# A four-layer graph network on one core: the softmax sums of the attention layers by transposing records, and a bias moved into a norm's offset

## The chip, the core and the metric

The kernel runs on one core of one Trainium2 chip. The metric is device time in microseconds (us) of one execution; the smaller the better. Times before and after are medians of repeated runs. The profile is one further execution, recorded by the hardware profiler, and its own time stands beside those of the runs.

## The reference

Eight samples of 2048 nodes with 128 features go through four layers: two of masked multi-head attention with a feed-forward part (layers 0 and 1), and two graph attention layers (2 and 3). The mask is one 2048 x 2048 adjacency matrix with about 16 neighbours a node. The change touches layers 0 and 1 alone:

```python
Q = (h @ Wq).reshape(B, N, NUM_HEADS, HEAD_DIM)      # 8 heads of 16
K = (h @ Wk).reshape(B, N, NUM_HEADS, HEAD_DIM)
V = (h @ Wv).reshape(B, N, NUM_HEADS, HEAD_DIM)
scores = jnp.einsum('bnhd,bmhd->bhnm', Q, K) / jnp.sqrt(jnp.asarray(HEAD_DIM, jnp.float32))
scores = jnp.where(mask, -jnp.inf, scores)
attn = jax.nn.softmax(scores, axis=-1)
attn_out = jnp.einsum('bhnm,bmhd->bnhd', attn, V).reshape(B, N, OUT_DIM)
x = h + (attn_out @ Wo + bo)
x = _layer_norm(x, ln1_g, ln1_b)
y = jax.nn.relu(x @ W1 + b1) @ W2 + b2
x = _layer_norm(x + y, ln2_g, ln2_b)
```

Two facts of this formula are used by the change. The softmax needs, for each node, sample and head, the sum of the exponentials over the node's neighbours. And the second bias b2 is added to `x + relu(x @ W1 + b1) @ W2`: if b2 is added to x itself, through the offset of the first norm, then the same b2 enters `x @ W1` too, and b1 has to be made smaller by `W1.T @ b2`.

## The kernel before

**Preparation.** In the opening (`start`), VectorE sweeps the adjacency matrix in 16 blocks of 128 rows and finds each node's neighbours; nodes are then sorted by their number of neighbours. In the same sweep a generator `prepare` makes the weights ready, one step of it in some rounds of the sweep. For layers 0 and 1 it centres the output weights and the two biases (`centered`, L246 to L248) and splits each bias into three bf16 rows (`parts`, L233 to L239), so that one bf16 product with a matrix of ones (`ones_bf`) can add the bias to a whole bank of PSUM.

**Blocks and chunks.** After the sort, a block is 128 nodes with lists of nearly the same length. Block 0 has the longest lists, block 15 the shortest (`CAPS`: 29, 23, 21, ... 12, 10 slots). In layers 0 and 1 a chunk is two slots of a block: two gathers by the GpSimd queue (L294) fetch, for each of the 128 nodes, the rows of two neighbours with keys and values of all eight samples. There are 282 chunks in the two layers, two of them "folded" (the few longest lists of block 0, spread over all partitions). A chunk goes through these steps, each of them a step of the generator `attention_chunk`:

1. VectorE multiplies keys by the query (L627).
2. VectorE adds halves of the products (L633); TensorE turns and adds them into the tile `pair` (L308, eight records); ScalarE takes the exponential (L649) into one slot of a ring of `RING` = 8 tiles, `ring`. It lies there with the weights' (slot, sample, head) index on the partitions and the nodes along the row.
3. TensorE turns the weights back (`back`, L653), ScalarE copies them (L657). At the last chunk of a block, or when six chunks have gathered, `block_sums` runs.
4. VectorE multiplies values by the weights (L665).
5. and 6. TensorE adds the turned values of the two slots into the accumulator `acc` (L308, eight records each).

**The sums of weights, before.** `block_sums` takes the exponentials of the chunks that have gathered and multiplies each by `fold_slots`, a matrix that is two unit matrices of 64 on top of each other. This turns a chunk's weights and adds its two slots in one fp32 product with 64 columns of output (L605). If the block has had sums before, they lie in `partial` and are added by a product with the unit matrix. At the block's last chunk ScalarE copies the sums to `block_sum` (L609), takes their logarithm (L616), and starts the generator `scales`: an exponential of the negative logarithm, spread over the 16 features of a head (L695), eight transposes by TensorE and two copies by ScalarE (L706). `scale` is then one over the sum, in the layout of the accumulator.

**The order of the work.** Nothing is scheduled by a planner: the program writes the order of all engines by hand. The loop in `layers` goes over all chunks. In the round of chunk i it issues, in this order: step 3 of chunk i-1; step 6 of the chunk weighed in the round before; then step 1 of chunk i, a slot, step 2 of chunk i, a slot; then `weigh` with steps 4 and 5 of chunk i-2 (and before them `sums`, if that was the last chunk of its block); then one more slot. A slot advances every waiting generator by one step: the scales, the tails of blocks that are done, the loading of lists, and the fetching of gathers. Four slots after the last chunk of a block was weighed, `outputs` multiplies the accumulator by `scale` on VectorE (L688), and two halves of a tail (`attention_tail`) follow as generators among the next chunks.

**The tail.** For four samples at a time: the product with the output weights, the first bias and the residual (L719, L724, L728), a norm on ScalarE, four transposes, the norm's gain and offset by ScalarE (`affine`, with two columns of `col`), the first feed-forward product (L741), its bias and ReLU on ScalarE (columns 4 and 5 of `col`), then into one bank `y`: the second bias by a bf16 product of 512 columns (L752), the centred residual (L757) and the second product (L762), which all accumulate; a second norm follows, transposes, and the projection of the next layer's rows (L511), which the GpSimd queue writes to the next layer's table.

Of the kernel before, what the change touches and what calls it, by code (L numbers as in the profile page):

```python
# [9 lines left out]
F32 = mybir.dt.float32  # L10
# [8 lines left out]
P = 128  # L19
B, N, D = 8, 2048, 128  # L20
NT = N // P
NH = 8
# [7 lines left out]
NB = 8  # L30
# [3 lines left out]
RING = 8  # L34
# [55 lines left out]
def sparse_path(ctx: ExitStack, tc: tile.TileContext, ins: dict, out: bass.AP, flag: bass.AP):  # L90
# [47 lines left out]
    fold_slots = const.tile([P, NB * NH], F32, name="fold_slots")  # L138
    nc.vector.tensor_add(fold_slots, ident[:, : NB * NH], ident[:, NB * NH :])
# [44 lines left out]
    def load(name, shape, src=None):  # L184
        t = const.tile(shape, F32, name=f"w_{name}")
        nc.scalar.dma_start(t, ins[name] if src is None else src)
        return t
# [17 lines left out]
    for l in (0, 1):  # L205
        W[l] = {
            "qkv": load(f"L{l}_qkv", [P, 384]),
            "o": load(f"L{l}_o", [P, D]),
            "1": load(f"L{l}_gnn_W1", [P, FF]),
            "2": load(f"L{l}_w2", [P, 2, D]),  # L210
            "col": load(f"L{l}_col", [P, 6]),
            "row": row(f"L{l}_row", 4 * D).rearrange("p (a b) -> p a b", b=D),
        }
# [36 lines left out]
    def prepare():  # L250

        for l in (0, 1):
            w = W[l]
            nc.vector.tensor_scalar_mul(w["qkv"][:, :D], w["qkv"][:, :D], 0.25)
            centered(w["o"])
            row_z, row_y = w["row"][:, 0, :], w["row"][:, 1, :]
            centered(row_z)
            w["row_z"] = parts(row_z, f"z{l}")
            yield
            for f in range(2):  # L260
                centered(w["2"][:, f, :])
            centered(row_y)
            w["row_y"] = parts(row_y, f"y{l}")
            yield
        for l in (2, 3):
            w = W[l]
            pa = pair
            nc.tensor.matmul(pa[:, :2], w["T"], w["col"][:, 2:4], start=True, stop=True)
            yield
            nc.vector.tensor_copy(w["h"][:, D : D + 2], pa[:, :2])  # L270
            centered(w["h"][:, :D])
# [323 lines left out]
    def block_sums(l, t, box, last):  # L595

        assert written[0] - box["exps"][0][2] < RING
        terms = [(e, fold_slots[: e.shape[0], :]) for e, folded, _ in box["exps"] if not folded]
# [4 lines left out]
        ps = misc()[:, : NB * NH]  # L603
        for i, (a, b) in enumerate(terms):
            nc.tensor.matmul(  # L605
                ps, a, b, start=i == 0, stop=i + 1 == len(terms), skip_group_check=True
            )
        if last:
            nc.scalar.copy(block_sum[:, t, :], ps)  # L609
        else:  # L610
            box["partial"] = small.tile([P, NB * NH], F32, tag="partial", name="partial")
            nc.scalar.copy(box["partial"], ps)
        box["exps"].clear()
        if last:
            box["r"] = small.tile([P, NB * NH], F32, tag="logs", name="logs", bufs=1)
            nc.scalar.activation(box["r"], ps, AF.Ln)  # L616
            threads.append(scales(l, box))

    def attention_chunk(l, c):
# [41 lines left out]
        if c["last"] or len(box["exps"]) == RING - 2:  # L661
            block_sums(l, t, box, c["last"])
# [12 lines left out]
    def sums(l, t, box):  # L675
        if l < 2:
            if t == NT - 1:
# [35 lines left out]
    def attention_tail(l, t, box, i):  # L713
# [25 lines left out]
        for f in range(2):  # L739
# [12 lines left out]
        nc.tensor.matmul(  # L752
            y, ones_bf, wt["row_y"][:, None, :].to_broadcast([P, 4, D]),
            start=True, stop=False, skip_group_check=True,
        )
        for j in range(4):
            nc.tensor.matmul(  # L757
                y[:, j, :], n1T[:, j, :], center, start=False, stop=False,
# [348 lines left out]
    for l in range(4):  # L1107
        per = 2 if l < 2 else 4
        for t, k, ns, folded in pieces(l, per):
# [3 lines left out]
            every.append(c)  # L1113
    now = [0, 0]
# [630 lines left out]
def layouts(inputs):  # L1745
# [5 lines left out]
    for l in (0, 1):  # L1751
        w = {k: a[f"L{l}_gnn_{k}"] for k in _ATTN}

        def heads_last(m):
# [6 lines left out]
            [w["ln1_g"], w["ln1_b"], w["ln2_g"], w["ln2_b"], w["b1"][:P], w["b1"][P:]], axis=1  # L1761
# [34 lines left out]
```

## Time and profile before

| what | us |
|---|---|
| median of 3 runs | 2945.51 (2943.55 to 2946.8) |
| the profiled execution | 2833.26 |
| its span, first to last instruction | 2831.5 |
| opening: sweep, sort, first rows | 0 to about 165 |
| layers 0 and 1 | about 165 to 1918 |
| layers 2 and 3 | about 1918 to 2831 |

The profiled execution is the one in which all durations of this text were recorded; sums of such durations are set against its time, not against the median. In the lists of the profile, a line has the source line, the engine (PE is TensorE's products, PEld its loading of weights, DVE is VectorE, ACT is ScalarE, POOL is GpSimd), the operation, what it writes and reads, and how often; then the busy time, the mean duration of one in ns, and the idle time of the engine just before, with what ended it. In the timeline a line begins with the start and the duration in us. TensorE's durations overlap, since its records are pipelined: what one record costs is the distance from its start to the next one's.

### The profile page before, as it was taken

The page shows a single profiled execution, that of the slowest core. Times are in us where ns is not written, and L with a number is a line of the kernel's source. Part 1 is how long each engine was busy: PE and PEld are TensorE (multiplying, and loading weights), DVE is VectorE, ACT ScalarE, POOL GpSimd, SP SyncE. Part 2 cuts the span into 40 slices and gives each one's busy share as a digit, 9 for nine tenths or more (in the row PEclk, how much of TensorE's full clock was granted, in tenths as well). Part 3 has the DMA queues.
Part 4 walks back from the last instruction along what each step waited for, and adds up shares of the span by engine and source line. Part 5 has one row for each costly group of instructions (what it writes and reads, how often), then busy time and mean ns, then how long its engine had stood idle before and what let it go on. Part 6 is the DMA issues. An engine that isn't in the chain of part 4 may idle for free.

```text
span 2831.5 us, 49678 instructions
## 1 busy us (share of the span) xinstructions
PE 2394.6 (85%) x18176; PEld 2181.0 (77%) x18176; DVE 2520.7 (89%) x2496; ACT 1376.6 (49%) x5021; POOL 1749.0 (62%) x1276
## 2 busy tenths in 40 slices
PE   5867899898899998799989999998567787888885
PEld 4656888787888887688878888887567786787785
DVE  8888999998899896999999899986889997799995
ACT  3511444454455655154445555556346566354554
POOL 1267688678755554646565565563777775677772
PEclk9988999999999999999999999999789888999998
DMA  9698899999989888789999899985999999999994
GB/s 359 249 376 334 353 333 343 379 336 343 382 328 353 322 313 301 312 317 356 347 380 370 342 366 366 349 298 199 356 411 399 400 409 338 343 411 413 405 413 170
DMA packets 197765, 982.13 MB, mean 347 GB/s; under 512 B 30284, under 2 KB 32076, under 8 KB 125520
## 3 DMA queue, kind: packets, MB, share of 16 engines
q0 software_dynamic: 172112, 885.12, 81.2%
q1 hardware_dynamic: 20502, 75.52, 6.9%
q10 hardware_dynamic: 4900, 18.24, 1.7%
q8 instruction: 146, 2.39, 0.3%
q14 instruction: 105, 0.86, 0.1%
HBM read 921.35 MB, written 91.55 MB: 358 GB/s over the span
## 4 chain that ended last, share of the span: by engine, by line
PE 43%; DVE 22%; DMA 14%; issue 7%; ACT 7%; POOL 1%; POOLq 0%; DVEq 0%; ACTq 0%
PE acc L308 14%; DMA kv<-table,lists 11%; DVE kv L627 7%; DVE kv L665 7%; PE pair L308 4%; PE m L762 4%; PE m L741 4%; PE m L315 3%; PE m L511 3%; DVE kv L633 2%; PE m L757 2%; PE m L605 2%; PE m L564 2%; DVE kv L807 2%; PE m L724 2%
## 5 line engine op out<-in xcount | busy, mean ns | idle before, releaser
L294 POOL DMA_INDIRECT kv<-table,lists x938 | 1282.6, 1367 | 681.4 <-PE acc L308 343.4
L308 PE MATMUL acc<-ident,kv 128*128 128x128 f32 x8048 | 1057.5, 285 | 166.9 <-DVE kv L665 90.1
L308 PEld LDWEIGHTS acc<-ident,kv 128*128 128x128 f32 x8048 | 962.4, 149 | 233.9 <-DVE kv L665 114.2
L665 DVE TENSOR_TENSOR kv<-kv,weights 128x2048 f32<-128x2048 f32 (+1 forms) x282 | 626.5, 2222 | 73.0 <-ACT weights L657 72.9
L627 DVE TENSOR_TENSOR kv<-kv,q 128x2048 f32<-128x2048 f32 (+1 forms) x280 | 618.2, 2208 | 48.1 <-DMA kv<-table,lists 31.4
L807 DVE TENSOR_TENSOR kv<-kv,pair 128x3584 f32<-128x3584 f32 (+1 forms) x150 | 530.7, 3538 | 1.0
L308 PE MATMUL pair<-ident,kv 128*128 128x128 f32 (+1 forms) x2256 | 303.7, 279 | 76.4 <-issue 53.0
L633 DVE TENSOR_TENSOR kv<-kv 128x1024 f32<-128x1024 f32 (+1 forms) x282 | 334.8, 1187 | 9.1
L308 PEld LDWEIGHTS pair<-ident,kv 128*128 128x128 f32 (+1 forms) x2256 | 259.5, 142 | 96.1 <-issue 70.4
L294 POOL DMA_INDIRECT kv<-table,sorted_lists x150 | 191.6, 1277 | 147.4 <-PE acc L308 48.3
L657 ACT COPY weights<-pair 128x128 f32<-128x128 f32 (+1 forms) x282 | 73.3, 260 | 394.7 <-PE pair L653 389.5
L474 ACT ACTIVATE n<-m,eps 128x128 f32<-128x128 f32 x512 | 181.1, 370 | 146.3 <-PE m L762 142.0
L812 ACT ACTIVATE kv<-kv,ws 128x128 f32<-128x128 f32 x544 | 174.6, 397 | 155.6 <-DVE ws L801 145.9
L649 ACT ACTIVATE ring<-pair 128x128 f32<-128x128 f32 (+1 forms) x282 | 77.7, 276 | 316.1 <-PE pair L308 253.8
L849 ACT ACTIVATE n<-m,eps 128x128 f32<-128x128 f32 x256 | 90.6, 373 | 178.5 <-PE m L841 176.6
L762 PE MATMUL m<-w_L_w,hT 128*128 128x128 f32 x1024 | 156.3, 275 | 0.0
L481 ACT ACTIVATE n<-m,rs 128x128 f32<-128x128 f32 x512 | 145.9, 374 | 0.3
L741 PE MATMUL m<-n1T,w_L_gnn_W 128*128 128x512 f32 x256 | 133.7, 606 | 7.9 <-ACT hT L746 5.0
L498 POOL DMA_INDIRECT table<-rows,perm x57 | 94.8, 1663 | 68.7 <-ACT own L534 17.3
L762 PEld LDWEIGHTS m<-w_L_w,hT 128*128 128x128 f32 x1024 | 135.0, 192 | 0.0
L315 PE MATMUL m<-ident,n 128*128 128x128 f32 x640 | 114.2, 291 | 13.7 <-ACT n L481 7.4
L511 PE MATMUL m<-w_L_h,xT 128*128 128x130 f32 x512 | 84.8, 298 | 42.7 <-ACT xT L485 27.3
(220 smaller groups left out, 3702.4 us busy)
## 6 DMA issues: line engine op xcount, KB each, us to landing
kept<-xT SPq DMA_DIRECT2D x48, 512.0 KB, 7.2
xT<-kept SPq DMA_DIRECT2D x48, 512.0 KB, 7.1
kv<-in_adj_dram SPq DMA_DIRECT2D x16, 1024.0 KB, 8.8
table<-kv ACTq DMA_DIRECT2D x16, 1024.0 KB, 8.0
kv<-table,lists POOLq DMA_INDIRECT x938, 8.9
kv<-in_x_nodes_dram SPq DMA_DIRECT2D x16, 512.0 KB, 12.6
kv<-table,sorted_lists POOLq DMA_INDIRECT x150, 7.0
found<-cand POOLq DMA_DIRECT2D x16, 64.0 KB, 5.8
```

Source lines behind the costliest of these rows:

```text
L294: this = nc.gpsimd.indirect_dma_start(out=dst, out_offset=None, in_=tables[l][:, :] if need == NT else views[l][0], in_offset=bass.Indirec ...
L308: nc.tensor.matmul(dst, src, ident, start=start, stop=True, is_transpose=True, skip_group_check=True)
L315: nc.tensor.transpose(pt[:, j * P : (j + 1) * P], src[:, j, :], ident)
L474: nc.scalar.activation(dst[:, i, :], z[:, i, :], AF.Square, bias=eps, scale=D**-0.5, accum_out=ss[:, i : i + 1],)
L511: nc.tensor.matmul(pp[:, j, :], xT[:, h + j, :], w["qkv"][:, D:] if l < 2 else w["h"], start=j == 0, stop=True, skip_group_check=True,)
L627: nc.vector.tensor_mul(kk, kk, q[:, None].to_broadcast([P, ns, NB, D]))
L633: nc.vector.tensor_add(hk.rearrange("p j (c h) -> p c j h", h=NH), kj[:, :, :NH, :], kj[:, :, NH:, :])
L665: nc.vector.tensor_mul(vv, vv, w.rearrange("p (s b h) -> p (s b) h", b=NB, h=NH)[:, :, None, :] .to_broadcast([P, ns * NB, HD, NH]),)
L741: nc.tensor.matmul(ph, wt["1"][:, f * P : (f + 1) * P], n1T.rearrange("p b c -> p (b c)"), start=True, stop=True,)
L762: nc.tensor.matmul(y[:, j, :], hT[:, f, j, :], wt["2"][:, f, :], start=False, stop=f == 1, skip_group_check=True,)
L807: nc.vector.tensor_mul(hv[:, :, :nv, :], hv[:, :, :nv, :], wc[:, :, :nv, None].to_broadcast([P, ns, nv, D]))
L812: nc.scalar.mul(hv[:, i, b, :], hv[:, i, b, :], ws[:, i, b - nv : b - nv + 1])
```

## The change

The sums: `fold_slots` goes. `block_sums` now turns each chunk's weights by one transposing record with the unit matrix, into 128 columns, so that the two slots stay side by side; they accumulate in PSUM. It always ends in a copy to `partial`, now 128 columns wide. The halves of `partial` are added by VectorE in `sums`, which runs where the block's last chunk is weighed; the logarithm and the start of `scales` move there from `block_sums`. The ring has nine tiles in place of eight, so `block_sums` runs at seven chunks in place of six; it also runs whenever the next chunk belongs to another block (`leave`).

The bias: `prepare` no longer centres and splits the second bias. It takes b2 as a seventh column of `col`, computes `W1.T @ b2` by two small products into `pair`, subtracts it from the columns of b1 and adds b2 to the offset of the first norm. The bf16 product at the head of `y` goes.

```diff
-RING = 8
+RING = 9
...
-    fold_slots = const.tile([P, NB * NH], F32, name="fold_slots")
-    nc.vector.tensor_add(fold_slots, ident[:, : NB * NH], ident[:, NB * NH :])
...
-            row_z, row_y = w["row"][:, 0, :], w["row"][:, 1, :]
+            row_z = w["row"][:, 0, :]
             centered(row_z)
             w["row_z"] = parts(row_z, f"z{l}")
-            yield
+            pb = pair
+            for f in range(2):
+                nc.tensor.matmul(
+                    pb[:, f : f + 1], w["1"][:, f * P : (f + 1) * P], w["col"][:, 6:7],
+                    start=f == 0, stop=f == 1, skip_group_check=True,
+                )
+            yield
+            nc.vector.tensor_sub(w["col"][:, 4:6], w["col"][:, 4:6], pb[:, :2])
+            nc.vector.tensor_add(w["col"][:, 1:2], w["col"][:, 1:2], w["col"][:, 6:7])
             for f in range(2):
                 centered(w["2"][:, f, :])
-            centered(row_y)
-            w["row_y"] = parts(row_y, f"y{l}")
             yield
...
-    def block_sums(l, t, box, last):
+    def block_sums(t, box, last):
...
-        terms = [(e, fold_slots[: e.shape[0], :]) for e, folded, _ in box["exps"] if not folded]
+        plain = [e for e, folded, _ in box["exps"] if not folded]
+        terms = []
         if "partial" in box:
             terms.append((ident, box["partial"]))
         if last and t == 0:
             terms += [(merge, box["wf"][:, i, :]) for i in range(FOLD)]
-        ps = misc()[:, : NB * NH]
+        ps = misc()[:, :P]
+        for i, e in enumerate(plain):
+            m = e.shape[0]
+            nc.tensor.matmul(
+                ps[:, :m], e, ident[:m, :m], start=i == 0, stop=not terms and i + 1 == len(plain),
+                is_transpose=True, skip_group_check=True,
+            )
         for i, (a, b) in enumerate(terms):
             nc.tensor.matmul(
-                ps, a, b, start=i == 0, stop=i + 1 == len(terms), skip_group_check=True
-            )
-        if last:
-            nc.scalar.copy(block_sum[:, t, :], ps)
-        else:
-            box["partial"] = small.tile([P, NB * NH], F32, tag="partial", name="partial")
-            nc.scalar.copy(box["partial"], ps)
+                ps[:, : b.shape[-1]], a, b, start=False, stop=i + 1 == len(terms),
+                skip_group_check=True,
+            )
+        box["partial"] = small.tile([P, P], F32, tag="partial", name="partial")
+        nc.scalar.copy(box["partial"], ps)
         box["exps"].clear()
-        if last:
-            box["r"] = small.tile([P, NB * NH], F32, tag="logs", name="logs", bufs=1)
-            nc.scalar.activation(box["r"], ps, AF.Ln)
-            threads.append(scales(l, box))
...
-        if c["last"] or len(box["exps"]) == RING - 2:
-            block_sums(l, t, box, c["last"])
+        if c["last"] or c["leave"] or len(box["exps"]) == RING - 2:
+            block_sums(t, box, c["last"])
...
     def sums(l, t, box):
         if l < 2:
+            both = box["partial"]
+            nc.vector.tensor_add(block_sum[:, t, :], both[:, : NB * NH], both[:, NB * NH :])
+            box["r"] = small.tile([P, NB * NH], F32, tag="logs", name="logs", bufs=1)
+            nc.scalar.activation(box["r"], block_sum[:, t, :], AF.Ln)
+            threads.append(scales(l, box))
...
         y = misc().rearrange("p (b c) -> p b c", c=D)
-        nc.tensor.matmul(
-            y, ones_bf, wt["row_y"][:, None, :].to_broadcast([P, 4, D]),
-            start=True, stop=False, skip_group_check=True,
-        )
         for j in range(4):
             nc.tensor.matmul(
-                y[:, j, :], n1T[:, j, :], center, start=False, stop=False,
+                y[:, j, :], n1T[:, j, :], center, start=j == 0, stop=False,
                 skip_group_check=True,
             )
...
+    for c, n in zip(every, every[1:] + [None]):
+        c["leave"] = n is None or n["box"] is not c["box"]
...
-            [w["ln1_g"], w["ln1_b"], w["ln2_g"], w["ln2_b"], w["b1"][:P], w["b1"][P:]], axis=1
+            [w["ln1_g"], w["ln1_b"], w["ln2_g"], w["ln2_b"], w["b1"][:P], w["b1"][P:], w["b2"]],
+            axis=1,
```

More of the change, by code (lines that the diff above doesn't have):

```diff
@@ L210, in sparse_path @@
             "2": load(f"L{l}_w2", [P, 2, D]),
-            "col": load(f"L{l}_col", [P, 6]),
+            "col": load(f"L{l}_col", [P, 7]),
             "row": row(f"L{l}_row", 4 * D).rearrange("p (a b) -> p a b", b=D),
```

## The prediction

> **What bounds the kernel now.** I read the page first, then the table of stretches, then who waits for whom on VectorE (DVE) inside a stretch, then the timeline of one block's end.
>
> ```profile
> span 2831.5 us, 49678 instructions
> ...
> PE 2394.6 (85%) x18176; PEld 2181.0 (77%) x18176; DVE 2520.7 (89%) x2496; ACT 1376.6 (49%) x5021; POOL 1749.0 (62%) x1276
> ```
>
> Over the span DVE leads TensorE (PE) by a little. The change touches only the opening (0 to 165 us) and the two attention layers (165 to 1918 us), so those have to be read alone:
>
> ```profile
> 165.00:600.00 435.00, 365.99 (x2739) 331.63 (x2738) 413.72 (x336) 163.59 (x561) 321.26 (x196) 0.93 0.92 353
> ...
> 800.00:1055.00 255.00, 246.33 (x1915) 221.28 (x1915) 228.66 (x165) 145.82 (x498) 140.49 (x89) 0.99 0.90 340
> ...
> 1600.00:1918.00 318.00, 303.17 (x2470) 275.90 (x2469) 288.14 (x169) 181.91 (x697) 192.37 (x112) 1.00 0.91 345
> ```
>
> Columns: stretch, length, busy PE, PEld, DVE, ACT, POOL, granted clock, DMA share, GB/s. From 165 to 600 us DVE is busy 95% and PE 84%: a chunk costs DVE 2.29 + 1.22 + 2.30 us (L627, L633, L665). In the last blocks of each layer (800 to 1055, 1600 to 1918) PE is busy 97% and 95%, DVE 90%: lists are short there, and the tail, which costs PE the same for every block, weighs more. What DVE waits for in 800 to 1055:
>
> ```profile
> DVE kv L665 <- ACT weights L657: 20.2, 11, 4.1
> ...
> DVE o L688 <- PE acc L308: 1.2, 1, 1.2
> ```
>
> 20.2 us there, and 22.3 us in 1600 to 1918, go to weights that PE turns over late. That is all that a faster PE can win in these two stretches. One end of a block, on DVE:
>
> ```profile
> 934.87 1.23 DVE L665 TENSOR_TENSOR kv<-kv,weights 128x1024 f32<-128x1024 f32 x1 [1.75 <-ACT weights L657]
> 936.01 2.29 DVE L627 TENSOR_TENSOR kv<-kv,q 128x2048 f32<-128x2048 f32 x1
> 938.33 1.22 DVE L633 TENSOR_TENSOR kv<-kv 128x1024 f32<-128x1024 f32 x1
> 943.61 2.29 DVE L665 TENSOR_TENSOR kv<-kv,weights 128x2048 f32<-128x2048 f32 x1 [4.05 <-ACT weights L657]
> ...
> 949.28 1.28 DVE L688 TENSOR_TENSOR o<-acc,scale 128x512 f32<-128x512 f32 x2
> ```
>
> DVE waits 1.75 and 4.05 us for weights, then runs without a gap: PE is the bound up to 943, DVE from there until the next tail.
>
> [...] a product is two records, a transpose one, and records start equally far apart. [...] here 12 sums' records lie 107.5 ns apart and 8 transposes 109 ns:
>
> ```profile
> 1013.26 1.45 PE L605 MATMUL m<-fold_slots,ring 128*128 128x64 f32 x12
> 1014.55 1.04 PE L308 MATMUL acc<-ident,kv 128*128 128x128 f32 x8
> 1015.42 1.03 PE L308 MATMUL pair<-ident,kv 128*128 128x128 f32 x8
> ...
> 1017.06 0.38 PE L752 MATMUL m<-parts_y,ones_bf 128*128 128x512 bf16 x1
> 1017.28 0.39 PE L757 MATMUL m<-center,n1T 128*128 128x128 f32 x2
> ```
>
> [...] The trace has that shape once, at 215 ns:
>
> ```profile
> L139 DVE TENSOR_TENSOR fold_slots<-ident 128x64 f32<-128x64 f32 x1 | 0.2, 215 | 0.0
> ```
>
> **The change, part by part.**
>
> *PE, sums.* 280 chunks (282 less two folded) give 560 records; each becomes one: 560 x 107.5 - 280 x 109 ns = 29.7 us less. Partial sums: 30 products now. With a flush at seven chunks or on leaving a block, counted through the loops, 57 flushes take the place of 62 and 25 carry a partial: 60 x 108 - 50 x 111 ns, 0.9 us less.
>
> *PE, bias.* 64 L752 records go, each 0.22 us of PE (1017.06 to 1017.28): 14.2 us. In all 44.8 us of PE.
>
> *Where that counts.* In the block shown, PE loses 12 + 4 sum records (925.42 to 926.70 and 934.44 to 935.07, 1.91 us) and gains 7 (0.76), and loses two L752 (0.44): 1.6 us before the second wait. The eight transposes of scale (0.88 us), now ahead of it, move behind it. So the weights come 2.5 us earlier. Blocks 9 to 15 of layer 0 and 8 to 15 of layer 1, 15 in all, show such waits: at most 42.5 us, 2.8 a block. Elsewhere PE waits for DVE, L665 above all, and its gain is hidden by DVE's three products per chunk; if DVE were quicker it would count.
>
> *DVE, sums.* 32 adds of 128x64, 0.13 us (start to next start after L139) to 0.215 us each. In the 17 blocks where DVE is the bound they are on the path: 2.2 to 3.7 us, taken 3.5; in the others they lie inside the wait for weights. The add waits for ACT's copy of the partial; behind it in DVE's queue stands L665 of the same chunk, which needs weights copied about 1 us earlier. Where DVE leads, this costs L665 up to 1 us, but PE wants that product only 5 us later (946.58); I take 0, with 0 to 0.3 us a block for the range.
>
> *ACT.* 62 copies of 212 ns become 57 of 264 ns (L657's row, same shape): 1.9 us more on an engine at 49%, taken 0. Ln and the scale's Exp move from the step after the weights to the weighing step, over one chunk later. Ln waits for the DVE add, and ACT's queue behind it holds a tail's row copies; the add has long run, so no new wait there. No DMA moves; SP's and POOL's order is the same.
>
> *The wait that comes.* Scale used to be ready 5.2 us before L688 at 949.28. Now, counting from the turned weights at 942.55: the second row copies end about +3.7, Ln .23 and Exp 1.07 take it to +5; transposes at +5.1 to +5.5; the tail's projection, whose input sits behind Exp on ACT, to +7.3; the chunk's eight transposes .87, scale's second four .44, two ACT copies of .6 with a row copy between: about +10. L688 stood at +6.7, so it comes 3.4 us later from there, against 2.5 us gained: a net +0.9 in such a block. In layer 1, blocks 8 to 10, the weights' waits are 1.5 to 2.3 us and no projection lies in that chunk: scale is ready near +7.5, and about 1.5 us is kept. Between these I take 0.8 us kept a block: 15 x 0.8 = 12 us. Where DVE is the bound, 5.65 us of DVE work lie between L633 and L688 and scale needs 2.6 us: hidden.
>
> *Opening.* Centring and splitting the second bias runs on DVE from 43.53 to 46.21 us and again for layer 1, in a stretch where DVE has no gap: 5.4 us go. A subtraction and an addition of 2 and 1 columns (near L247's 150 ns) add 0.35 us a layer. Net 4.6 us. The subtraction waits for two new products; PE has a whole round of the sweep (6 us) for them: taken 0, up to 2 us a layer.
>
> *Between the layers* (1055 to 1300 us) the wait for weights is 21.1 us in six pieces, and q another 5.2; I take 3 us.
>
> Sum: -4.6 + 3.5 - 12 - 3 = -16 us against the profiled execution's 2833.3 us (span 2831.5): about 2817. The median of the runs, 2945.5, lies 4.0% above that execution; scaled alike, -16.7, about 2929. Why they differ the profile doesn't show: with a slower PE the gain would grow, with slower DMA shrink.
>
> **Rivals.**
>
> *PE's gain is kept whole.* For it: 42.5 us of waits name PE. Against it: scale's later place. 15 x 2.5 = 37 us in place of 12: -41, 2902.
>
> *Hidden.* DVE at 95% and DMA at 0.92 set the pace, scale's lateness eats the gain: -4.6 + 5.5 for all adds, about +1, 2946. For it: DVE runs gapless after 943. Against it: the 97% of PE.
>
> *Slower: scale comes late.* Its place is L688 in the 15 late blocks; it decides once the chain from the turned weights to scale's second copy passes about +9.2 us, where the 2.5 us are used up. At +11 each block loses 1.8 us: 27 us, with the other terms (-4.6 + 3.5 - 3) +23, 2969; at +10, +9, 2955. For it: my own count for the worst blocks is +10. Against it: layer 1's blocks, and transposes of scale that move into chunks where PE has less to do.
>
> *The change does not halve the records*: excluded nearly, since every transpose in the trace is one record.
>
> **How the numbers follow.** Chances: forecast 0.48, kept whole 0.2, hidden 0.16, slower 0.16. The range 2902 to 2952 holds the forecast with its bounds (scale, adds, the subtraction's wait), the whole gain, the hidden case, and part of the slower one. A measurement can tell about 0.2% (5.9 us) from no change: faster 0.69, same 0.15, slower 0.16.
>
> **What would show it.** Right: half as many sum records, no L752; DVE's wait for weights in the late blocks well under 42 us, and a new wait of L688 for scale, 1 to 3 us each in those blocks; the opening some 4 us shorter. Wrong: L688 waits over 4 us a block (slower), or none at all (kept whole); or L627 waiting for gathers instead.

## The result: 1.2% faster, twice the forecast

| | us |
|---|---|
| kernel before, median of 4 runs beside the changed one | 2944.53 (2941.18 to 2946.8) |
| changed kernel, median of 4 runs | 2910.26 (2906.23 to 2913.36) |
| ratio, with its 95% interval | 0.9884 (0.9867 to 0.9901) |
| the changed kernel's profiled execution, and its span | 2913.36, 2911.6 |

The change takes 34.3 us away; the forecast was 16.5, from 2945.5 to 2929. The sign was right and the result lies in the range, but the size was off by a factor of two. The terms for the opening and for the late blocks came out as forecast; one step, on the early blocks, had the mechanism wrong, and it makes up the whole difference.

The two profiled executions can't be set against each other by their spans: 2831.5 us before, 2911.6 after, although the runs say that the changed kernel is the faster one. The first experiment shows why: layers 2 and 3, which the change doesn't touch, took 895 us in the first trace of the kernel before and 1009 in its second. So everything below is read from the opening and the two attention layers, up to the product with `scale` of layer 1's last block (L688 before, L698 after). Its first half begins at 1936.8 us in the first trace of before, at 1935.1 in the second, and at 1901.3 in the trace after. The difference there is 33.8 or 35.5 us, as much as the runs show.

The changed kernel's busy times, then one group of instructions of the kernel before and three of the changed one:

```profile
PE 2406.4 (83%) x17830; PEld 2161.2 (74%) x17830; DVE 2521.9 (87%) x2507; ACT 1378.2 (47%) x5016; POOL 1714.2 (59%) x1276
```

```profile
L665 DVE TENSOR_TENSOR kv<-kv,weights 128x2048 f32<-128x2048 f32 (+1 forms) x282 | 626.5, 2222 | 73.0 <-ACT weights L657 72.9
```

```profile
L670 DVE TENSOR_TENSOR kv<-kv,weights 128x2048 f32<-128x2048 f32 (+1 forms) x282 | 626.1, 2220 | 24.5 <-ACT weights L662 14.4 <-ACT rs L468 9.0 <-ACT rs L469 1.1
L632 DVE TENSOR_TENSOR kv<-kv,q 128x2048 f32<-128x2048 f32 (+1 forms) x280 | 618.1, 2207 | 33.7 <-DMA kv<-table,lists 28.0 <-ACT q L573 5.7
...
L683 DVE TENSOR_TENSOR block_sum<-partial 128x64 f32<-128x64 f32 x32 | 7.6, 239 | 15.9 <-ACT partial L621 6.7 <-ACT weights L662 4.7 <-ACT n L478 2.3
```

TensorE has 346 instructions fewer (18176 before): 280 records of sums, 10 of partial sums and 64 bias products went, 8 records for the product of W1 and b2 came. VectorE has 11 more: 32 new adds, less what the opening lost. The product with the weights, L665 before and L670 now, waits 24.5 us in all, where it waited 73.0; the new add (L683) waits 15.9. The profile puts one product's wait down to now one, now another operation of ScalarE (`weights`, `rs`, `n`), the one that ended last, so waits are compared here by these totals of the waiting operation.

One of the stretches of the prediction (stretch, length, busy PE, PEld, DVE, ACT, POOL, granted clock, DMA share, GB/s):

```profile
800.00:1055.00 255.00, 243.16 (x1874) 214.92 (x1873) 229.76 (x169) 151.74 (x528) 136.98 (x86) 1.00 0.89 339
```

Here, in late blocks, TensorE is busy 95% where it was 97%, VectorE 90% as before. In the first stretch of the prediction, 165 to 600, the trace has the products with the weights of 71 chunks, where it had those of 70, and six of the new adds besides. That is a first hint that time was won where the prediction had none to win.

The end of the block that the prediction showed, on TensorE and then on VectorE (start, duration, and in brackets the idle time before it and what ended that):

```profile
916.88 1.08 PE L611 MATMUL m<-ident,ring 128*128 128x128 f32 x7
917.89 1.09 PE L312 MATMUL acc<-ident,kv 128*128 128x128 f32 x8
```

```profile
918.29 0.23 DVE L683 TENSOR_TENSOR block_sum<-partial 128x64 f32<-128x64 f32 x1 [0.73 <-ACT partial L621]
918.44 1.22 DVE L670 TENSOR_TENSOR kv<-kv,weights 128x1024 f32<-128x1024 f32 x1
...
925.18 2.29 DVE L670 TENSOR_TENSOR kv<-kv,weights 128x2048 f32<-128x2048 f32 x1 [2.06 <-ACT rs L468]
...
932.64 0.69 DVE L698 TENSOR_TENSOR o<-acc,scale 128x512 f32<-128x512 f32 x1 [1.70 <-ACT scale L716]
```

Seven turns take 1.01 us from 916.88 to the next record at 917.89 (the prediction had 0.76), in place of 12 + 4 records before. The two waits for weights of 1.75 and 4.05 us have become a wait of 0.73 for the partial sums and one of 2.06. And the wait that the prediction announced is there: L698 waits 1.70 us for the second half of `scale`.

In the opening, two operations of 0.15 us with no wait ahead of them (L264 and L265, at 43.46 and 43.53 us) stand where centring and splitting the second bias took 2.7 us.

### The profile page after: what moved, and what is told of

Its sections match the earlier page's. It is cut to its first block, busy times and chain, and to the rows that moved or that the text cites. A ratio compares the mean times of both kernels' runs of the same rounds, so it can differ in the third digit from the quotient of the medians.

```text
span 2911.6 us, 48942 instructions
## 1 busy us (share of the span) xinstructions
PE 2406.4 (83%) x17830; PEld 2161.2 (74%) x17830; DVE 2521.9 (87%) x2507; ACT 1378.2 (47%) x5016; POOL 1714.2 (59%) x1276
## 5 line engine op out<-in xcount | busy, mean ns | idle before, releaser
L298 POOL DMA_INDIRECT kv<-table,lists x938 | 1268.0, 1352 | 785.8 <-PE acc L312 343.2
L312 PE MATMUL acc<-ident,kv 128*128 128x128 f32 x8048 | 1097.3, 289 | 210.5 <-issue 93.5
L312 PEld LDWEIGHTS acc<-ident,kv 128*128 128x128 f32 x8048 | 980.1, 150 | 294.0 <-issue 148.7
L670 DVE TENSOR_TENSOR kv<-kv,weights 128x2048 f32<-128x2048 f32 (+1 forms) x282 | 626.1, 2220 | 24.5 <-ACT weights L662 14.4
L632 DVE TENSOR_TENSOR kv<-kv,q 128x2048 f32<-128x2048 f32 (+1 forms) x280 | 618.1, 2207 | 33.7 <-DMA kv<-table,lists 28.0
L824 DVE TENSOR_TENSOR kv<-kv 128x1024 f32<-128x1024 f32 x75 | 91.6, 1222 | 70.9 <-ACT kv L818 56.8
L698 DVE TENSOR_TENSOR o<-acc,scale 128x512 f32<-128x512 f32 x128 | 83.3, 684 | 67.0 <-PE acc L312 29.2
```

The lines of the kernel that those rows point to most:

```text
L298: this = nc.gpsimd.indirect_dma_start(out=dst, out_offset=None, in_=tables[l][:, :] if need == NT else views[l][0], in_offset=bass.Indirec ...
L312: nc.tensor.matmul(dst, src, ident, start=start, stop=True, is_transpose=True, skip_group_check=True)
L632: nc.vector.tensor_mul(kk, kk, q[:, None].to_broadcast([P, ns, NB, D]))
L670: nc.vector.tensor_mul(vv, vv, w.rearrange("p (s b h) -> p (s b) h", b=NB, h=NH)[:, :, None, :] .to_broadcast([P, ns * NB, HD, NH]),)
```

## The experiments

The theory after the result: **TensorE's time counts in every block, not in the late ones alone**, because TensorE makes the query and the weights that VectorE waits for, and perhaps because it frees the buffers that the next gathers need. The rivals: the surplus comes from the sums' new order or from the ring's ninth tile; or from the bias; or it is no gain of the attention layers at all, but of layers 2 and 3. Four sets of kernels were run, each set on one chip with the kernel before beside it. Ratios are to that kernel before, and "the mark" is the start of the last block's L688 or L698 of layer 1 in the trace.

### The kernel before, once more (before_again)

No edit; one run with its profile.

> The kernel before, unchanged, for a second trace of it. The first trace is 4% shorter than the timed runs, and its layers 2 and 3 took 895 us from the last L688 of layer 1 to the end, those of the changed kernel 1010 us. Theory: the difference between the profiled execution and the runs lies in layers 2 and 3 alone, so this trace has its last L688 of layer 1 near 1937 us again and ends near 2942 us. Rival: the two attention layers are slower too in ordinary runs, and that L688 comes near 1970 us or later; then the gain read between the first two traces is not the gain of the runs.

It took 2946.34 us, with a span of 2944.5. The mark lies at 1935.1 us, 1.7 from the first trace's. Layers 2 and 3 in the first trace of before, then in the second:

```profile
1918.00:2831.00 913.00, 701.51 (x5446) 664.29 (x5444) 777.49 (x924) 471.58 (x1855) 601.33 (x565) 0.89 0.92 359
```

```profile
1918.00:2944.00 1026.00, 753.54 (x5440) 691.23 (x5440) 777.38 (x922) 469.23 (x1849) 589.75 (x564) 0.84 0.87 319
```

The same work of VectorE (777 us) takes 113 us longer, with TensorE at a lower granted clock (0.84 against 0.89). So the 4% between the first profile and the median, which the prediction could not explain, lie in layers 2 and 3. Two traces of one kernel differ by up to 2 us at the mark; single stretches between blocks differ by up to 3.5.

### The two halves, each alone (bias_alone, sums_alone)

The first has the bias's part of the change and the old sums. The second has the new sums, with the old ring of eight, and keeps the bias product.

```diff
 bias_alone
-        nc.tensor.matmul(
-            y, ones_bf, wt["row_y"][:, None, :].to_broadcast([P, 4, D]),
...
 sums_alone
-            nc.tensor.matmul(
-                ps, a, b, start=i == 0, stop=i + 1 == len(terms), skip_group_check=True
-            )
+            nc.tensor.matmul(
+                ps[:, :m], e, ident[:m, :m], start=i == 0, stop=not terms and i + 1 == len(plain),
+                is_transpose=True, skip_group_check=True,
+            )
...
```

> Only the second bias is moved; the sums stay as before. Theory (TensorE's time counts in nearly every block, because its backlog also delays the gathers): 14.2 us of PE records and 4.6 us of DVE in the opening go, about 2.6 us of the opening and 9 us of the rest are won: 2933 us (-12). Rival of the prediction (PE's time counts only in the 15 late blocks): -2.6 and 15 x 0.44 = 6.6 us: 2935. Rival that it is the sums which matter alone: -3.

> Only the sums are changed, with a ring of eight tiles (flush at six chunks), and the bias product stays. Theory: 30.6 us of PE go, and about two thirds of it are won, -20 us: 2924. Rival of the prediction (late scales give most of it back, nothing in blocks that DVE bounds): -8 to +4 us: 2937 to 2948.

The bias alone took 2922.15 us beside 2944.11, ratio 0.9935 (0.9915 to 0.9955), the sums alone 2927.96, ratio 0.9938 (0.9914 to 0.9962). At the mark they are 17.0 and 16.3 us ahead of before_again; together 33.3, against 33.8 for the whole change. The halves simply add up.

The opening is worth 4.7 us of it. To the first product with `scale` it is 269.2 us, the mean of the eight traces with the bias's part and the tail in its place (after, bias_alone, ring8, pe_twice, dve_five, pe_early, pe_late and scales_at_once), and 273.9 in the three without (the two of before, and sums_alone). So 12.3 of the bias's 17.0 us were won in the attention layers, where it takes away 64 products of 0.22 us, 14.2 in all. A change that only removes TensorE time there kept most of it, and 34 of the 64 products belong to the 17 blocks where the prediction had put TensorE's gain down as hidden. The gain is not spread evenly: against before_again it is 0.9 us up to block 8 of layer 0, which is within the scatter of single stretches, and 6.2 us up to block 8 of layer 1.

### The ring with eight tiles (ring8)

```diff
-RING = 9
+RING = 8
```

> The changed kernel with eight ring tiles: block_sums runs at six chunks again, 4 or 5 more partial sums of two records each per layer (1.1 us of PE a layer) and an ACT copy of 264 ns each. Both theories: within 0.1% of the changed kernel (2910), at most +3 us. If the burst of seven turns is what helps, it is slower by more than 5 us.

2911.21 us beside 2944.11, ratio 0.9888 (0.9848 to 0.9927), the mark at 1899.3: as the changed kernel. The ninth tile, and with it the number of flushes, brings nothing that can be seen.

### TensorE's gain given back (pe_twice)

Every turn of the sums is issued twice, the second time starting the accumulation anew. This adds 280 records, at 109 ns each 30.5 us.

```diff
-        for i, e in enumerate(plain):
+        for i, e in enumerate(plain + plain):
...
-                ps[:, :m], e, ident[:m, :m], start=i == 0, stop=not terms and i + 1 == len(plain),
+                ps[:, :m], e, ident[:m, :m], start=i % len(plain) == 0,
+                stop=not terms and i + 1 == 2 * len(plain),
```

> The changed kernel with every transposing record of the sums issued twice (the second round overwrites the first, so the result is the same): 280 more records of 109 ns, 30.5 us of PE, with the order and the late scales of the changed kernel. Theory (PE's time counts nearly everywhere, the gathers' buffers included): two thirds of it come back, +20 us: 2930, and L632's wait for gathers and L670's for weights rise to those of before. Rival of the prediction (PE counts only in the 15 late blocks, about 1 us each): +12 to +15 us in the late blocks and nothing before block 8 of layer 0.

2934.89 us beside 2944.38, ratio 0.9968 (0.9951 to 0.9985). The mark comes 25.3 us later than in the changed kernel, for 30.5 us of records at 109 ns, or 34.6 by their busy time in the trace (77.6 us where the changed kernel has 43.0). Of this, 10.0 us lie between block 0 and block 8 of layer 0, where the prediction had TensorE hidden. This kernel also says what the sums' new order costs: its TensorE has the load of bias_alone, and its mark comes 8.5 us after bias_alone's (1926.6 and 1918.1). So of the sums, some 25 us are won by fewer records and some 8.5 are given back by the adds, the later scales and what follows from them, each known to the 2 us by which two traces of one kernel differ.

### Four more adds a block (dve_five)

```diff
+            for _ in range(5):
-            nc.vector.tensor_add(block_sum[:, t, :], both[:, : NB * NH], both[:, NB * NH :])
+                nc.vector.tensor_add(block_sum[:, t, :], both[:, : NB * NH], both[:, NB * NH :])
```

> The changed kernel with the add of the halves issued five times: 128 more adds of 0.13 us (issue distance) to 0.215 us on DVE. If DVE is the bound in 17 of 32 blocks, as the prediction says, half of them are on the path: +9 to +15 us, 2920 to 2925. Theory now (DVE had gaps of 1 to 6 us a block there too, which end with PE or a gather): the first adds vanish in gaps, +4 to +9 us, 2914 to 2919. If DVE is the bound in all blocks: +17 to +27 us.

2932.07 us beside 2944.38, ratio 0.9966 (0.9951 to 0.9981); the mark is 21.3 us later than in the changed kernel. Five adds in succession cost more than the expectation allowed, as the end of one block shows:

```profile
922.86 1.27 DVE L684 TENSOR_TENSOR block_sum<-partial 128x64 f32<-128x64 f32 x5 [0.73 <-ACT partial L621]
924.04 1.22 DVE L670 TENSOR_TENSOR kv<-kv,weights 128x1024 f32<-128x1024 f32 x1
```

From 922.86 to the next product it is 1.18 us, where the single add took 0.15 (918.29 to 918.44): 0.26 us for each added one. Over the trace their starts lie 0.25 to 0.32 us apart, so that the 128 adds are 33.7 us of VectorE, not 17 to 27, and 63% of them arrive at the mark (78% with the opening left out, which in this trace came out 4.3 us shorter). They arrive by stage: 9.0 us up to block 8 of layer 0 and 9.3 up to block 8 of layer 1, for 8.4 us of adds in each; 6.3 us in the late blocks of layer 1 and none in those of layer 0, for 7.4 us in each. So VectorE is on the path in the early blocks, as the prediction said. What it had wrong is that TensorE was not. (The logarithm takes the last add's result, so that scale may come up to 1 us later too, an estimate from four adds of 0.26 us; that part is not told apart.)

### TensorE loaded in the early or in the late blocks (pe_early, pe_late)

This is the test of the step itself. Blocks 0 to 7 of both layers, or blocks 8 to 15, get 336 more records, 36.6 us at 109 ns each.

```diff
+        times = 3 if t < 8 else 1
-        for i, e in enumerate(plain):
+        for i, e in enumerate(plain * times):
```

For pe_late the first line reads `times = 4 if t >= 8 else 1`.

> The changed kernel with the sums' transposing records of blocks 0 to 7 of both layers issued three times: 168 chunks, 336 more records of 109 ns, 36.6 us of TensorE, all in the blocks that the prediction called bound by DVE. If DVE hides TensorE's time there (the prediction): at most 5 us slower than the changed kernel, ratio to before 0.988 to 0.990. If TensorE's time counts there too (what pe_twice suggests): 25 to 37 us slower, ratio 0.997 to 1.001.

> The same amount of TensorE in the other half: records of blocks 8 to 15 of both layers issued four times, 112 chunks, 336 more records, 36.6 us. Both the prediction (a PE-bound stage) and the theory of pe_twice expect most of it on the path: 28 to 37 us slower than the changed kernel, ratio to before 0.998 to 1.001. If the wait for scale is what sets these blocks, more: over 37 us.

By the busy time of these records in the traces the load is more than 36.6 us: 43 in pe_early and 39 in pe_late (82.3 us where the changed kernel has 43.0). The changed kernel, then pe_early:

```profile
L611 PE MATMUL m<-ident,ring 128*128 128x128 f32 (+1 forms) x280 | 43.0, 279 | 0.0
```

```profile
L612 PE MATMUL m<-ident,ring 128*128 128x128 f32 (+1 forms) x616 | 86.1, 280 | 0.0
```

| | us, before 2927.74 | ratio | mark, later than the changed kernel |
|---|---|---|---|
| pe_early | 2917.29 | 0.9959 (0.9937 to 0.9982) | 22.9 of 36.6 to 43 us |
| pe_late | 2931.07 | 1.0008 (0.9991 to 1.0025) | 38.9 of 36.6 to 39 us |

The ratios say the same as the marks: set against 0.9884, they are 22 and 36 us. In the late blocks all of TensorE's time counts; in the early ones 53 to 63% of it, with 12.8 us more up to block 8 of layer 0 and 9.8 up to block 8 of layer 1. Neither "hidden" (5 us or less) nor "the whole" describes the early blocks.

The added records stand directly ahead of VectorE's add, so a rival is that they cost time only through that place, which the kernel before did not have. In pe_early it is not so. Its groups, to be set beside those of the changed kernel above:

```profile
L634 DVE TENSOR_TENSOR kv<-kv,q 128x2048 f32<-128x2048 f32 (+1 forms) x280 | 618.0, 2207 | 48.3 <-DMA kv<-table,lists 25.9 <-ACT q L573 16.5 <-PE pair L660 2.6
L672 DVE TENSOR_TENSOR kv<-kv,weights 128x2048 f32<-128x2048 f32 (+1 forms) x282 | 626.0, 2220 | 32.9 <-ACT weights L664 16.3 <-ACT rs L468 9.4 <-ACT rs L469 6.0
...
L685 DVE TENSOR_TENSOR block_sum<-partial 128x64 f32<-128x64 f32 x32 | 7.4, 233 | 16.5 <-ACT partial L623 14.1 <-ACT rs L468 2.3
```

The add waits 16.5 us in place of 15.9. What grew is the wait of the product with the query (from 33.7 to 48.3 us, though the gathers' share of it fell from 28.0 to 25.9) and of the product with the weights (from 24.5 to 32.9): VectorE waits for things that TensorE now makes later. In pe_late the place does matter; there the add waits 29 us more than in the changed kernel:

```profile
L685 DVE TENSOR_TENSOR block_sum<-partial 128x64 f32<-128x64 f32 x32 | 7.5, 235 | 45.1 <-ACT partial L623 30.7 <-issue 5.1 <-ACT rs L469 4.6
```

### The tail placed a slot later (outputs_later)

```diff
-range(4 if l < 2 else 3 if t > NT - 4 else 5)
+range(5 if l < 2 else 3 if t > NT - 4 else 5)
```

> The changed kernel with one more yield ahead of outputs: L688's successor (L698) then stands behind the next weights' product L670 on DVE, not ahead of it. In the changed trace DVE waits 26.8 us at L698 for scale, 9.9 of it at the change of layers. Theory (the wait is idle time of DVE that PE's late blocks mostly hide): the wait falls under 8 us and the time by 3 to 10 us: 2900 to 2907. Rival (the tail starts one slot later and its burst on PE moves into the next block): no gain or up to +10 us: 2910 to 2920.

If late scales cost much, giving them one slot more should help. 2948.59 us beside 2944.38, ratio 1.0018 (1.0002 to 1.0034), and the mark 37.8 us later than in the changed kernel. VectorE's waits in the two attention layers, the changed kernel first, then this one:

```profile
DVE o L698 <- ACT scale L716: 26.8, 18, 9.9
...
DVE kv L632 <- ACT q L573: 5.7, 6, 1.9
```

```profile
DVE kv L670 <- ACT weights L662: 37.8, 16, 7.0
DVE kv L632 <- ACT q L573: 33.0, 14, 4.5
...
DVE o L698 <- ACT scale L716: 9.6, 9, 1.7
```

The wait for scale fell from 26.8 to 9.6 us, as intended. But the wait for the query grew by 27 us, and that of the product with the weights from 24.5 us to 37.8. That the tail's work now meets the query's and the weights' on TensorE and ScalarE is argued from this, not tested.

### Scale started at once, and the tail sooner (scales_at_once, outputs_sooner, both_sooner, before_sooner)

scales_at_once takes the generator's first step where it is made, so that the exponential stands one slot earlier. outputs_sooner puts the tail one slot earlier; both_sooner does both; before_sooner does it in the kernel before.

```diff
 scales_at_once
-            threads.append(scales(l, box))
+            turning = scales(l, box)
+            next(turning)
+            threads.append(turning)
 outputs_sooner, before_sooner
-range(4 if l < 2 else 3 if t > NT - 4 else 5)
+range(3 if l < 2 else 3 if t > NT - 4 else 5)
```

> The changed kernel with the first step of the scales (ScalarE's Exp) issued in the weighing step itself and not in the slot after it, so that the whole chain to scale comes one slot sooner. In the changed trace DVE waits 26.8 us at L698 for scale. Theory (late scales cost part of the gain): that wait falls below 15 us and the time by 4 to 10 us, 2900 to 2906. Rival (scale's lateness is hidden behind other waits, or its transposes now stand on TensorE ahead of an Exp that is not done): within 3 us of the changed kernel, or up to 10 us slower.

> The changed kernel with one yield less ahead of outputs, so L698 and the tail come one slot sooner. One slot later cost 38 us, mostly as waits of L632 for the next block's query. Theory A (the tail's burst on TensorE must be clear of the query's products): sooner is better, L632's waits for q vanish (5.7 us) and 3 to 10 us are won unless L698 waits for scale. Theory B (scale is ready only just before L698 now): L698's wait rises by about 2 us in each of the 15 late blocks and the kernel is 10 to 30 us slower than the changed one, 2920 to 2940.

> Scales one slot sooner and outputs one slot sooner together. If the lateness of scale (theory B) is all that hurts outputs_sooner, this one is as fast as the changed kernel or up to 10 us faster, 2900 to 2912. If the place of the tail itself hurts, it is slower than the changed kernel like outputs_sooner.

> The kernel before with one yield less ahead of outputs; its scale is ready 5 us ahead of L688, so no wait for scale comes in. It shows what the place of the tail is worth by itself. Theory A: 3 to 10 us faster than before (2934 to 2941). Theory B: L688 waits for the last accumulation instead in the late blocks (it waits 8 us already), 0 to 15 us slower.

| | us, before 2832.05 | ratio |
|---|---|---|
| scales_at_once | 2801.15 | 0.9878 (0.9849 to 0.9908) |
| outputs_sooner | 2879.76 | 1.0162 (1.0139 to 1.0186) |
| both_sooner | 2883.67 | 1.0169 (1.0147 to 1.0192) |
| before_sooner | 2882.47 | 1.0163 (1.0137 to 1.0188) |

On this chip layers 2 and 3 ran as in the first trace, so the times stand some 110 us lower; the ratios are what is compared. scales_at_once is the changed kernel again (its interval holds 0.9884, and its mark is 2.2 us earlier). Its wait for scale, then the totals of the weights' product and of the add:

```profile
DVE o L700 <- ACT scale L718: 25.2, 12, 9.4
```

```profile
L670 DVE TENSOR_TENSOR kv<-kv,weights 128x2048 f32<-128x2048 f32 (+1 forms) x282 | 626.0, 2220 | 25.9 <-ACT weights L662 25.8
...
L683 DVE TENSOR_TENSOR block_sum<-partial 128x64 f32<-128x64 f32 x32 | 7.6, 237 | 17.2 <-ACT partial L621 17.2
```

Scale is waited for 12 times in place of 18, but for nearly as long, 25.2 us after 26.8; the other two totals were 24.5 and 15.9. So moving the exponential alone does not bring scale sooner where it is waited for, and the 8.5 us that the new order costs were not won back. Which part of them is the add's wait and which is scale's stays open.

The other three lose 1.6 to 1.7%, with or without the earlier scale, and in the kernel before as well. There, again the waits of VectorE in the attention layers, before_again first, then before_sooner:

```profile
DVE kv L665 <- ACT weights L657: 47.3, 32, 6.9
DVE kv L665 <- ACT rs L464: 16.8, 6, 4.1
...
DVE kv L627 <- ACT q L569: 12.7, 8, 3.3
```

```profile
DVE kv L665 <- ACT weights L657: 78.9, 34, 4.5
DVE kv L627 <- ACT q L569: 63.1, 19, 5.4
```

The query's wait is five times as long; that of the product with the weights, of which before_again has 6.5 us more under another name, grew from 70.6 to 78.9 us. For the changed kernel four slots is the best of the three places tried: one slot sooner it loses 2.9% (1.0162 over the 0.9878 of scales_at_once), one slot later 1.4% (1.0018 over 0.9884).

## What the prediction had right, and the step that failed

**The working, term by term**, against the trace after (time between the products with `scale`, L688 or L698), from the first trace of before, on which the prediction was built, and from the second:

| term | predicted, us | from the first trace | from before_again |
|---|---|---|---|
| opening | -4.6 | -2.6 (-4.7 over the eleven traces named above) | -0.5 |
| 17 blocks "where DVE is the bound" | +3.5 | -9.9 (layer 0), -6.6 (layer 1) | -13.4, -5.0 |
| 15 late blocks | -12 | -5.6 (layer 0), -6.8 (layer 1) | -4.0, -6.9 |
| between the layers | -3 | -4.0 | -4.0 |
| sum | -16 | -35.5 | -33.8 |

The stretches are not quite the prediction's blocks: block 0 lies in the opening or between the layers, and block 8 of layer 1 among the early ones. With it among the late ones, layer 1 reads -5.9 and -7.6 from the first trace, which changes nothing of what follows.

Apart from the 17 blocks, the terms lie within about 2 us of the forecast. **The failed step** is the sentence "Elsewhere PE waits for DVE, L665 above all, and its gain is hidden by DVE's three products per chunk", and the +3.5 us drawn from it. In place of a loss of 3.5 us these blocks gave 16.5 (18.4 from before_again): the term was 20 us too high, which is the whole surplus. TensorE's time there was not hidden; pe_early puts the part that counts at 53 to 63%. The rival of a gain "kept whole" meant something else, 37 us from the late blocks alone; those gave 12.4, and that the total came near that rival's was luck.

Why the step failed is to be read in the same profile. The prediction read 95% busy as "the bound" and listed VectorE's waits in the late blocks only. Up to block 8 of layer 1, before and after, they are these:

```profile
DVE kv L665 <- ACT weights L657: 15.8, 9, 5.0
DVE kv L627 <- ACT q L569: 8.0, 6, 1.9
```

```profile
DVE kv L632 <- ACT q L573: 5.4, 5, 1.9
DVE kv L670 <- ACT weights L662: 3.9, 3, 2.3
DVE o L698 <- ACT scale L716: 2.9, 1, 2.9
DVE block_sum L683 <- ACT rs L468: 2.2, 1, 2.2
```

23.8 us of waiting for things that TensorE makes stood in blocks that the prediction had called VectorE's. After, the same two products wait 11.2 us (1.8 of it under `rs`), the add 2.2 and the product with scale 2.9, 16.3 in all; the stretch got shorter by 6.6. One list of waits more would have shown that there was something to win.

In layer 0 the early blocks are less plain. Up to block 8, before and after:

```profile
DVE kv L627 <- DMA kv<-table,lists: 12.5, 13, 1.7
...
DVE kv L627 <- PE pair L308: 3.1, 2, 2.0
```

```profile
DVE kv L632 <- DMA kv<-table,lists: 7.8, 6, 2.4
```

VectorE waits mostly for gathers, and that wait fell by 4.7 us, the one for `pair` by 3.1. It is tempting to say that TensorE's sums free the buffers of the gathers sooner: the issue of the gathers waits 27.8 us for `acc` before and 24.1 after. The runs don't bear this out. In pe_twice, with the records given back, VectorE waits 14.7 us for gathers, but the issue waits only 20.6 for `acc`; and VectorE's wait for gathers is 11.7 us in ring8, which has the load of the changed kernel, 4.9 in sums_alone, which has more, and 10.0 in pe_early, which has most. What does go with the sums' records is the total of VectorE's waits there: 12.3 to 18.1 us in the traces with single turns and the tail in its place (after, ring8, scales_at_once, dve_five, sums_alone, and pe_late, which adds turns in block 8 alone), 21.5 to 26.2 in those with the old sums or turns added throughout (both traces of before, bias_alone, pe_twice, pe_early). By which wait the time comes in layer 0 stays open.

The stretches between the marks, before (the four lines run from block 0 to 8 and from 8 to 15 of layer 0, then of layer 1) and after:

```profile
274.20:759.60 485.40, 437.29 (x3344) 396.80 (x3344) 458.10 (x375) 227.20 (x780) 374.57 (x226) 0.96 0.92 352
759.60:1079.20 319.60, 303.97 (x2332) 270.82 (x2332) 278.32 (x201) 183.21 (x632) 166.79 (x105) 0.99 0.87 329
1208.60:1639.00 430.40, 399.09 (x3112) 364.45 (x3113) 404.03 (x234) 212.79 (x807) 247.62 (x146) 0.96 0.92 351
1639.00:1936.80 297.80, 278.04 (x2231) 250.08 (x2230) 269.89 (x165) 170.92 (x649) 179.68 (x106) 0.99 0.90 340
```

```profile
271.50:747.00 475.50, 426.22 (x3250) 383.47 (x3250) 458.31 (x382) 226.83 (x780) 369.06 (x225) 0.96 0.93 357
747.00:1061.10 314.10, 297.82 (x2285) 263.87 (x2286) 279.74 (x209) 183.20 (x631) 169.80 (x106) 0.99 0.90 342
1186.50:1610.30 423.80, 387.44 (x3030) 349.70 (x3030) 404.91 (x242) 213.54 (x807) 231.08 (x147) 0.96 0.93 358
1610.30:1901.30 291.00, 272.27 (x2156) 242.75 (x2157) 271.25 (x172) 171.47 (x645) 171.52 (x105) 0.99 0.91 346
```

In the early blocks VectorE's busy time stays (458.1 and 458.3; 404.0 and 404.9 us), and the stretches get shorter by 9.9 and 6.6 us: what went is VectorE's idle time, 27.3 to 17.2 us in layer 0. TensorE's busy time fell there by 11.1 and 11.7 us, of which 73% arrived; in the late blocks it fell by 6.2 and 5.8, and 12.4 us arrived. (TensorE's busy time is no exact measure of its records' cost: the changed kernel's 280 turns are 43.0 us by it, and 30.5 at 109 ns each. So the shares are rough.) pe_early and pe_late found 53 to 63% and all of it, in the other direction.

In the early blocks VectorE is the engine that is busy most, 94% of 485.4 us up to block 8 of layer 0, where TensorE's products take 90% and its weight loads 82%, and dve_five agrees: VectorE's time counts there. VectorE's gaps lead to what TensorE makes: plainly in layer 1, where all 23.8 us of listed waits are for it. pe_early agrees too: 53 to 63%. The prediction went by the busiest engine there, and by VectorE's gaps only in the late blocks.

**What else was right.** The records did halve and the bias products went. The wait of the weights' product in 800 to 1055 and 1600 to 1918 fell, from 42.5 us to 11.0. The new wait of L698 for scale came, 1.70 us in the block shown, and but for the last block of layer 0 none reached the 4 us at which the change would have lost. VectorE's wait for weights in blocks 8 to 15 of layer 0 before, and its waits after:

```profile
DVE kv L665 <- ACT weights L657: 29.1, 14, 6.9
```

```profile
DVE o L698 <- ACT scale L716: 20.1, 12, 9.9
DVE kv L670 <- ACT rs L468: 4.1, 2, 2.1
DVE block_sum L683 <- ACT partial L621: 3.7, 4, 1.5
DVE kv L670 <- ACT weights L662: 2.5, 1, 2.5
DVE block_sum L683 <- ACT weights L662: 1.4, 1, 1.4
```

The weights' product and the add wait 11.7 us (the last four lines), where weights were waited for 29.1 us before. Of the 17.4 us won, 10.2 went into eleven waits for scale. The twelfth, 9.9 us at the end of the layer, took the place of a wait of 5.6 for `acc`. With the smaller waits counted, VectorE's idle time fell by 6.9 us (319.6 less 278.3, and 314.1 less 279.7), its busy time grew by 1.4, and 5.5 were kept. So more than half of what TensorE gave there did go into the wait for scale, as foretold.

**What was a little off.** The new wait was to be 1 to 3 us in each late block; the eleven are 0.9 us on average, and in the late blocks of layer 1 only four waits came, 3.4 us together. The add's wait for the partial sums was taken as 0; it is 15.9 us in all, eleven times, but it stands where the wait for weights stood, and the two together (40.4 us) are well below the 73.0 of before. The 42.5 us were not all that a faster TensorE could win in the two stretches: 7.1 us of waiting for `block_sum` and 2.4 for `acc` stood there besides. In the late blocks of layer 1 the term's parts were off both ways: the wait for weights fell from 19.3 us to 4.4, but the add took 8.5, so that 6.4 us were won where the prediction had 2.5 a block, and scale took far less than it had. That the term of the late blocks fits as a sum is in part luck. The slower rival, scale coming late by more than the weights gained, did not occur. That the time before was 4% above the profile's was carried into the forecast by scaling; it had nothing to do with the change.

## What to carry to other kernels

VectorE was busy 94 and 95% of the early stretches here and yet was not the bound of all of them: list an engine's waits in every stretch before calling another engine's gain hidden. TensorE at 90% and VectorE at 94% passed each chunk back and forth, and time on either counted in good part (in the early blocks 53 to 63% of TensorE's added records, and all of VectorE's added adds, 18.3 us for 16.8). Compare the total wait of the waiting operation, since the name that a wait is put down to changed between two traces of one kernel: of the weights' product, 72.9 us under `weights` in the first of before, 47.3 under `weights` and 23.3 under `rs` in the second. And when an edit moves work within a hand-written order, try the neighbouring places by themselves: one slot cost 1.6% in the kernel before, more than the whole change brings.

## What the runs showed of the hardware

The same program took 2832.05 us (median of 7) on one chip and 2944.38 (median of 46) on another, and the traces put such a gap into layers 2 and 3 alone, while the attention layers of the two traces of before agree within 2 us. From the mark to the end, the four traces from the first of these chips take 898 to 899 us, with a granted clock of 0.89 to 0.90; the nine from the three other chips take 994 to 1013 us, at 0.84 to 0.85. The kernels differ, but not in these layers. TensorE's records into `acc` there, first trace of before, then before_again (count, busy us, mean ns, idle us before them and why):

```profile
L308 PE MATMUL acc<-ident,kv 128*128 128x128 f32 x3758 | 474.1, 289 | 79.5 <-DVE kv L818 45.2 <-DVE kv L807 21.9 <-issue 8.1
```

```profile
L308 PE MATMUL acc<-ident,kv 128*128 128x128 f32 x3752 | 509.8, 295 | 131.3 <-issue 95.0 <-DVE kv L818 30.1 <-DVE kv L665 3.1
```

In the slower trace 95 us of idle time stand ahead of them in which TensorE waited for nothing that the profile shows, 8.1 in the other, and its granted clock in this stretch is 0.84 against 0.89. Which of the two is the cause, if either, is not settled; a gain is to be measured beside the kernel before on the same chip.
